# Fifth list tiles of two experts in one stage: 96 rows each, on four column groups of 32 and then on two halves

## The chip, the cores and the metric

The kernel runs on one core of one Trainium2 chip. A core has TensorE (matmuls, whose results go to PSUM banks), VectorE, ScalarE, GpSimd (POOL) and SyncE (SP), which work side by side and wait for each other by semaphores. Transfers are issued from SP's and POOL's queues. The metric is the device time of the whole kernel in microseconds (us); lower is better.

## The reference

The kernel computes two layers on 1024 tokens of 1024 channels. Layer 0 is a convolution-like attention with group norm, layer 1 is causal attention with 16 heads and then a mixture of 8 experts. The change is in the mixture alone:

```python
gate_logits = softmax(x @ gate_w + gate_b)
selected = (gate_logits >= THRESHOLD)            # 0.1
weights = gate_logits * selected
weights = weights / where(wsum == 0, 1, wsum)
for e in range(E):                               # 8 experts
    out = out + weights[:, e:e + 1] * (x @ expert_w[e] + expert_b[e])
```

`x` has 1024 rows, `expert_w[e]` is 1024 x 1024, all in f32. A token counts for an expert only where its gate is at least 0.1. With the reference's own inputs the experts get 560, 592, 542, 569, 578, 552, 545 and 538 of the 1024 tokens; of the first 896 tokens, experts 0 and 7 get 487 and 470.

## The kernel before

**Lists.** After the attention and the router, the kernel makes a list of token numbers for every expert (`gather`, `slot`, `add`, L693 to L695). It computes an expert only for the tokens on its list, in tiles of 128 entries. Five tiles are handled by the main path, `SLOTS = 5 * P` = 640 entries. Experts 0 and 7 (`SHORT`) have lists of the first 896 tokens, of which four tiles are handled; the last 128 tokens are computed for these two densely (`dense` L1135, `last_pe` L1207). If any list is longer (`most_i`, compared with `SLOTS` at L1219), a loop at the end computes what is left, all experts one after another. Unused entries at the end of a list point to tokens that aren't selected, with weight zero.

**One tile.** `get` / `fetch` (L712, L1060) issues four indirect gathers on POOL's queue, each bringing a quarter of a row into 128 partitions, into one of three `xg` buffers. `put` / `turn` (L724, L1063) transposes the tile on VectorE in blocks of 32. After the products, VectorE adds the bias, ScalarE multiplies by the gate weights, and `add_rows` (L743) issues an indirect transfer on POOL's queue that adds the rows to the output in DRAM.

**Pairs of tiles.** Tiles 0 and 1, and 2 and 3, are a pair of 256 rows. `products` (L1079) multiplies a pair by the expert's 1024 x 1024 weights with seven block products instead of eight (Strassen's scheme in Winograd's form). Each product is four matmuls of 128 x 128 by 128 x 512 (L1093). It needs sums of row blocks, `row_sums` (L1074, four VectorE operations, the last one in place: the block a21 becomes a11 - a21), and sums of weight blocks, which are made once per expert: `first_sum` and `second_sum` before its first pair, `third_sum` (in place in the weights: b12 becomes b22 - b12) and `fourth_sum` in it. The weights lie in two halves of 512 output columns, `w[e][0]` and `w[e][1]`; even and odd experts have buffers of their own (`w_even`, `w_odd`).

**The fifth tile.** For experts 1 to 6 the fifth tile has a stage of its own, `left_over` (L1117), between the products of the expert before and its own first pair. It multiplies the tile with the plain weights, in `weighted` (L731): for each half, eight matmuls of 128 x 128 by 128 x 512 (L737). It runs before `third_sum` changes the weights. While TensorE is in it, VectorE makes the fourth weight sum, the transpose of tile 1 and the row sums of the first pair.

**What sets the order.** This part is written out by hand (`manual_schedule`, L1126): the program order is each engine's order. `between` is a table of what is issued after the n-th product of a pair. So the stretch in which an expert's second pair is multiplied also transposes the next expert's first tiles and makes its first two weight sums. `load(e + 1)` is issued on SP's queue at the start of expert e, behind the stage `left_over(e)`, and waits there until the weights' buffers are free. A bias comes behind it, in the middle of the second pair, into one buffer. POOL's gathers and adds share one queue in program order.

Of the kernel before, what the change touches and what calls it, by code (L numbers as in the profile page):

```python
# [28 lines left out]
F32 = mybir.dt.float32  # L32
# [6 lines left out]
P = 128  # L39
# [18 lines left out]
NEG = -1e29  # L58
THRESHOLD = 0.1
Q = 4  # L60
SLOTS = 5 * P
SHORT = (0, E - 1)


# [1 line left out]
def kernel(  # L66
# [80 lines left out]
    def sums_of_A(a11, a12, a21, a22, s1, s2, s4):  # L147
        nc.vector.tensor_add(s1, a21, a22)
        nc.vector.tensor_sub(s2, s1, a11)
        nc.vector.tensor_sub(s4, a12, s2)  # L150
        nc.vector.tensor_sub(a21, a11, a21)

    def layer_norm(ln, t, dst):

# [300 lines left out]
    with ExitStack() as attention:  # L455
# [20 lines left out]
        def sums_of_B():  # L476
            nc.vector.tensor_sub(T[0], b12, b11)
            nc.vector.tensor_sub(T[1], b22, T[0])
            nc.vector.tensor_sub(b12, b22, b12)
            nc.vector.tensor_sub(T[2], b21, T[1])  # L480

        n_products = 0
# [221 lines left out]

        return w_tile(f"{name}{e}_{r}", expert_w[e][:, ts(r, HALF)], home=home)

    def expert_bias(e, home, name="w_e"):
        bias = home.tile([P, C], F32, tag="bias", name=f"{name}_bias{e}", bufs=1)
        nc.sync.dma_start(bias, expert_b[e].partition_broadcast(P))
        return bias  # L710

    def fetch(e, k, home, name="w_e", bufs=None):  # L712

        row = home.tile([P, Q, C // Q], F32, tag="xg", name=f"{name}_xg{e}_{k}", bufs=bufs)
        for g in range(Q):
            nc.gpsimd.indirect_dma_start(  # L716
                out=row[:, g, :],
                out_offset=None,
                in_=table[: (TOK - P) * Q, :] if e in SHORT else table,
                in_offset=bass.IndirectOffsetOnAxis(ap=gather[:, e, k * Q + g : k * Q + g + 1], axis=0),  # L720
            )
        return row

    def turn(row_T, row):  # L724

        nc.vector.transpose(  # L726
            row_T.rearrange("p c (g j) -> p g c j", g=Q),
            row.rearrange("p g (c i) -> p g c i", c=NC),
        )

    def weighted(gate, row_T, w, bias, home, name, between={}):  # L731
# [8 lines left out]
            nc.scalar.mul(y[:, ts(j, HALF)], y[:, ts(j, HALF)], gate)  # L740
        return y

    def add_rows(e, k, y):  # L743
        nc.gpsimd.indirect_dma_start(  # L744
            out=out[: TOK - P, :] if e in SHORT else out,
            out_offset=bass.IndirectOffsetOnAxis(ap=add[:, e, k : k + 1], axis=0),
            in_=y,
            in_offset=None,
            compute_op=ALU.add,
        )  # L750

    def by_rows(e, tiles, w, bias, home, name):

        tiles = list(tiles)

        def turned(k, row):
            row_T = home.tile([P, NC, P], F32, tag="row_T", name=f"{name}_xg_T{e}_{k}", bufs=3)
            turn(row_T, row)
            return row_T

        fetched = [fetch(e, k, home, name) for k in tiles[:2]]
        ready = [turned(tiles[0], fetched[0])]
        for n, k in enumerate(tiles):
            if n + 2 < len(tiles):
                fetched.append(fetch(e, tiles[n + 2], home, name))
            if n + 1 < len(tiles):
                ready.append(turned(tiles[n + 1], fetched[n + 1]))
            add_rows(e, k, weighted(slot[:, e, 1, k : k + 1], ready[n], w, bias, home, f"{name}{e}_{k}"))

    with ExitStack() as gating:  # L770
        l2, l2w = pool(gating, "l2"), pool(gating, "l2w", 2)
# [234 lines left out]
        def last_lists(entries):  # L1006
            read_lists(1, E, entries)


            pn = tr("pn")  # L1010
            nc.tensor.matmul(pn[:, :E], ones, kept, start=True, stop=True)
            need = l2.tile([P, E], F32, tag="need", name="need")
            nc.vector.tensor_copy(need, pn[:, :E])
            pn0 = tr("pn0")
            nc.tensor.matmul(pn0[:, :2], ones, kept_short, start=True, stop=True)
            nc.vector.tensor_scalar(need[:, :: E - 1], pn0[:, :2], float(P), None, ALU.add)
            most = l2.tile([P, 1], F32, tag="most", name="most")
            nc.vector.tensor_reduce(most, need, AX.X, ALU.max)
            nc.vector.tensor_copy(most_i, most)
# [11 lines left out]
        def half(e, j, l):  # L1031
            return w[e][l][:, 4 * j : 4 * j + 4, :]
# [15 lines left out]
        def third_sum(e):  # L1048

            T3[e] = half(e, 0, 1)  # L1050
            if e == E - 1:
                free = w_even.tile([P, NC, HALF], F32, tag="w", name="free")
                T3[e] = free[:, : NC // 2, :]
                last_rows.append(free[:, NC // 2 : NC // 2 + 2, :].rearrange("p a b -> p (a b)"))
            nc.vector.tensor_sub(T3[e], half(e, 1, 1), half(e, 0, 1))

        row = {}
        last = SLOTS // P - 1

        def get(e, k):  # L1060
            row[e, k] = fetch(e, k, two, bufs=3)

        def put(e, k):  # L1063

            if k == last:
                A[e, k] = l2w.tile([P, NC, P], F32, tag="row_T", name=f"one{e}", bufs=3)
                turn(A[e, k], row[e, k])
            else:
                pair, i = divmod(k, 2)
                if i == 0:  # L1070
                    A[e, pair] = two.tile([P, 2, NC, P], F32, tag="A", name=f"A{e}_{pair}")
                turn(A[e, pair][:, i, :, :], row[e, k])
# [6 lines left out]
        def products(e, pair, between):  # L1079
# [34 lines left out]
            rows_out(1, 0)  # L1114
            add_rows(e, 2 * pair + 1, y[1])

        def left_over(e):  # L1117

            between = {0: lambda: (fourth_sum(e), put(e, 1), get(e, 3)), 1: lambda: row_sums(e, 0)}
            get(e, 2)  # L1120
            y = weighted(slot[:, e, 1, last : last + 1], A[e, last], w[e], bias[e], l2w, f"one{e}", between)
            add_rows(e, last, y)

        with tc.manual_schedule():  # L1126
# [23 lines left out]
            )  # L1150
            get(0, 3)
            for e in range(E):
                if e not in SHORT:
                    left_over(e)
                if e + 1 < E:
                    load(e + 1)
# [6 lines left out]
                if e == 0:  # L1163
                    between[2] = lambda: (stage(3, NT - 1), fourth_sum(0), put(0, 2))
                    between[3] = lambda: (entries.append(copy_lists(1)), put(0, 3))
                    between[4] = lambda: (last_lists(entries[0]), row_sums(0, 1))
                    between.pop(1)
                elif e == E - 1:
                    between[0] = lambda: (third_sum(e), get(e, 3))
                    between[1] = lambda: (fourth_sum(e), put(e, 2))  # L1170
                if e + 1 < E - 1:
                    between[5] = lambda: get(e + 1, last)
                    between[6] = lambda: get(e + 1, 0)
                elif e + 1 == E - 1:
                    between[5] = lambda: get(e + 1, 0)
                    between[6] = lambda: get(e + 1, 1)
                products(e, 0, between)
                between = {}
                if e + 1 < E - 1:
                    between = {  # L1180
                        1: lambda: (bias.update({e + 1: expert_bias(e + 1, l2w)}), put(e + 1, last)),
                        2: lambda: (put(e + 1, 0), get(e + 1, 1)),
                        4: lambda: first_sum(e + 1),
                        5: lambda: second_sum(e + 1),
                        6: lambda: bias_step(e + 1),
                    }
                elif e + 1 == E - 1:
                    between = {
                        1: lambda: (bias.update({e + 1: expert_bias(e + 1, l2w)}), put(e + 1, 0), get(e + 1, 2)),
                        2: lambda: put(e + 1, 1),  # L1190
                        3: lambda: row_sums(e + 1, 0),
                        4: lambda: first_sum(e + 1),
                        5: lambda: second_sum(e + 1),
                        6: lambda: bias_step(e + 1),
                    }
                else:
                    between = {
                        1: lambda: nc.sync.dma_start(last_rows[0], out[ts(NT - 1, P), :]),
                        4: lambda: nc.vector.scalar_tensor_tensor(
                            last_rows[0], bias[e], gated[NT - 1][0][:, e, 1:2], last_rows[0], ALU.mult, ALU.add  # L1200
                        ),
                    }
# [16 lines left out]
    with tc.If(count > SLOTS), ExitStack() as rest:  # L1219
        w_rest, l3 = pool(rest, "w_rest", 4), pool(rest, "l3", 3)  # L1220
        for e in range(E):
            w_e = [half_weights(e, r, w_rest, "w_r") for r in range(2)]
            tiles = range(SLOTS // P - 1, NT - 1) if e in SHORT else range(SLOTS // P, NT)
            by_rows(e, tiles, w_e, expert_bias(e, l3, "w_r"), l3, "w_r")


# [57 lines left out]
```

## Time and profile before

| what | value |
| --- | --- |
| median of 3 runs | 1308.68 us (1306.49 to 1309.3) |
| the profiled execution, its own time | 1310.25 us |
| its span (first to last instruction) | 1308.4 us |
| TensorE busy | 1286.6 us, 98% |
| VectorE busy | 664.3 us, 51% |
| POOL busy | 344.3 us, 26% |
| ScalarE busy | 245.3 us, 19% |
| chain that ended last | TensorE 93%, VectorE 4%, rest 3% |
| the experts, first product to the end | from 821.8 us to the end of the span |
| fifth tiles on TensorE (L737, one_pe) | 83.4 us, 192 records |

A group's row gives line, engine, operation, result <- operands, shapes and count, then the time in which at least one of its instructions ran and the mean time of one, and then the idle time before them with what ended it. For a matmul, 128*32 is the stationary operand (128 partitions, 32 columns) and 128x512 what comes out of the moving columns. Times of one matmul contain its latency, and matmuls overlap: the busy time divided by the count is nearer to what one costs in a row of them. An f32 matmul leaves two records. In the timeline and the chain, the first column is the start in us from the start of the span and the second the length. The tiles `p` are the pairs' products, `one_pe` the fifth tile's, `w_e_xg` a gathered tile, `A` and `one` transposed ones, `S` and `T` the sums.

### The profile page before, as it was taken

To read this page: it belongs to the slowest core of one execution; us is meant where nothing else is said; L and a number is where in the kernel's file an instruction comes from. 1 tells how busy PE (TensorE), PEld (TensorE's weight loads), DVE (VectorE), ACT (ScalarE), POOL (GpSimd) and SP (SyncE) were. 2 spreads that over 40 slices of the span, in tenths; PEclk is the share of its full clock that TensorE was granted. 3 is DMA by queue.
4 is the path that set the end of the run, shared out by engine and by line. 5 is a ranking of instruction groups with operands and counts; after the bars stand their busy time and mean duration, and the time that the engine had idled before them with its cause. 6 is when DMAs were issued, how large, how long until landed. Compare 5 with 4: busy or idle time off the path is not lost.

```text
span 1308.4 us, 12324 instructions
## 1 busy us (share of the span) xinstructions
PE 1286.6 (98%) x4550; PEld 695.5 (53%) x4550; DVE 664.3 (51%) x1250; ACT 245.3 (19%) x572; POOL 344.3 (26%) x365
## 2 busy tenths in 40 slices
PE   9999999998999999999999998999999999999998
PEld 5445894777884555555554544444444444444443
DVE  5874220566323555554444755655646465555642
ACT  3200111330001333333323322111111111110110
POOL 0000060230000211111111113445454544453530
PEclk9999999998999999999999998999999999999999
DMA  9020023512201202010505215374757566555532
GB/s 350 2 65 17 1 76 92 203 65 81 65 18 46 65 1 65 1 65 1 193 17 196 96 65 201 73 220 115 214 124 190 147 164 174 145 165 140 111 75 58
DMA packets 61042, 136.12 MB, mean 104 GB/s; under 512 B 5905, under 2 KB 20257, under 8 KB 60977
## 3 DMA queue, kind: packets, MB, share of 16 engines
q1 hardware_dynamic: 47664, 94.32, 20.7%
q0 software_dynamic: 13312, 40.96, 14.4%
q8 instruction: 38, 0.62, 0.2%
q14 instruction: 28, 0.22, 0.1%
HBM read 97.51 MB, written 33.55 MB: 100 GB/s over the span
## 4 chain that ended last, share of the span: by engine, by line
PE 93%; DVE 4%; POOL 1%; DMA 1%; issue 1%; ACT 0%; DVEq 0%; ACTq 0%; POOLq 0%
PE p L1093 28%; PE pqk L489 15%; PE po L646 8%; PE pq L257 7%; PE pv L489 7%; PE one_pe L737 6%; PE pT L376 3%; PE py L441 2%; PE pk L319 2%; PE pc L340 2%; PE pv L401 2%; PE sc L573 2%; PE pst L617 2%; PE pa L627 2%; PE last_pe L1209 1%; POOL w_e_xg L716 1%
## 5 line engine op out<-in xcount | busy, mean ns | idle before, releaser
L716 POOL DMA_INDIRECT w_e_xg<-rows,gather x152 | 159.2, 1048 | 69.1 <-issue 42.0
L1093 PE MATMUL p<-w_e,A 128*128 128x512 f32 x368 | 164.6, 597 | 1.8 <-DVE slot L954 1.8
L605 POOL TENSOR_TENSOR s<-s,total 128x256 f32<-128x256 f32 x64 | 51.5, 826 | 346.4 <-DVE total L602 338.4
L1093 PEld LDWEIGHTS p<-w_e,A 128*128 128x128 f32 x368 | 70.4, 192 | 90.5 <-issue 88.6
L646 PE MATMUL po<-w_p,y_T 128*128 128x512 f32 x256 | 116.1, 598 | 0.0
L744 POOL DMA_INDIRECT out_dram<-y,add x32 | 60.8, 1899 | 205.7 <-ACT y L1099 133.1
L1093 PE MATMUL p<-T,S 128*128 128x512 f32 x256 | 112.7, 592 | 0.0
L1099 ACT ACTIVATE y<-y,slot 128x512 f32<-128x512 f32 x64 | 46.2, 722 | 341.3 <-DVE y L1107 172.5
L257 PE MATMUL pq<-w_q,xn 128*128 128x512 f32 x224 | 99.6, 596 | 1.4 <-DVE q_s L261 1.1
L489 PE MATMUL pqk<-ln,w_qk 128*128 128x512 f32 x192 | 85.0, 592 | 0.0
L737 PE MATMUL one_pe<-w_e,one 128*128 128x512 f32 x192 | 83.4, 592 | 0.0
L1093 PEld LDWEIGHTS p<-T,S 128*128 128x128 f32 x256 | 48.6, 190 | 60.8 <-issue 60.7
L646 PEld LDWEIGHTS po<-w_p,y_T 128*128 128x128 f32 x256 | 46.3, 190 | 49.1 <-issue 48.7
L257 PEld LDWEIGHTS pq<-w_q,xn 128*128 128x128 f32 x224 | 41.8, 190 | 51.8 <-issue 47.4
L726 DVE STREAM_TRANSPOSE A<-w_e_xg 128x1024 f32<-128x1024 f32 x32 | 39.7, 1241 | 51.4 <-DMA w_e_xg<-rows,gather 51.4
L737 PEld LDWEIGHTS one_pe<-w_e,one 128*128 128x128 f32 x192 | 36.5, 190 | 45.9 <-issue 45.7
L595 ACT ACTIVATE s<-s,top 128x256 f32<-128x256 f32 (+1 forms) x128 | 56.6, 443 | 18.1 <-DVE top L593 18.0
L489 PEld LDWEIGHTS pqk<-ln,w_qk 128*128 128x128 f32 x192 | 35.9, 190 | 42.1 <-issue 41.1
L489 PE MATMUL pqk<-T,S_qk 128*128 128x512 f32 x128 | 57.7, 593 | 0.0
L1093 PE MATMUL p<-w_e,S 128*128 128x512 f32 x128 | 57.5, 592 | 0.0
L1093 PE MATMUL p<-T,A 128*128 128x512 f32 x128 | 57.5, 592 | 0.0
L618 ACT COPY s_T<-pst 128x384 f32<-128x384 f32 x64 | 27.5, 481 | 157.6 <-PE pst L617 157.6
(256 smaller groups left out, 1801.0 us busy)
## 6 DMA issues: line engine op xcount, KB each, us to landing
w_e<-in_expert_w_dram SPq DMA_DIRECT2D x16, 2048.0 KB, 12.1
w_qk<-in_W_attnT_dram SPq DMA_DIRECT2D x8, 1024.0 KB, 6.4
xn<-in_xT_dram SPq DMA_DIRECT2D x8, 512.0 KB, 7.8
x_at<-in_x_dram SPq DMA_DIRECT2D x8, 512.0 KB, 7.1
w_v<-in_W_attnT_dram SPq DMA_DIRECT2D x2, 2048.0 KB, 11.8
x_rows<-x_at SPq DMA_DIRECT2D x8, 512.0 KB, 2.7
w_p<-in_W_projT_dram SPq DMA_DIRECT2D x2, 2048.0 KB, 8.4
xb<-x_rows SPq DMA_DIRECT2D x8, 512.0 KB, 6.8
```

The costliest lines, as they stand in the source:

```text
L257: nc.tensor.matmul(pq, xn[:, c, ts(t, P)], w_q[kc][:, c, :], start=(c == 0), stop=(c == NC - 1))
L376: nc.tensor.matmul(out_T[:, g, :, :], window[:, kc, :, :].rearrange("p i j -> p (i j)"), q0[:, kc, first : first + n_i, nj, :], start=(kc ...
L489: nc.tensor.matmul(bank, stationary(c), moving(c), start=(c == 0), stop=(c == NC // 2 - 1))
L595: nc.scalar.activation(s[:, h, cols], s[:, h, cols], AF.Exp, bias=top[:, qt, h : h + 1], accum_out=total[:, qt, h : h + 1],)
L605: nc.gpsimd.tensor_mul(s[:, :, cols], s[:, :, cols], total[:, qt, :].unsqueeze(2).to_broadcast([P, 2, (qt + 1) * P]),)
L646: nc.tensor.matmul(po, y_T[:, c, ts(t, P)], w_p[j][:, c, :], start=(c == 0), stop=(c == NC - 1))
L716: nc.gpsimd.indirect_dma_start(out=row[:, g, :], out_offset=None, in_=table[: (TOK - P) * Q, :] if e in SHORT else table, in_offset=bass.I ...
L726: nc.vector.transpose(row_T.rearrange("p c (g j) -> p g c j", g=Q), row.rearrange("p g (c i) -> p g c i", c=NC),)
L737: nc.tensor.matmul(pe, row_T[:, c, :], w[j][:, c, :], start=(c == 0), stop=(c == NC - 1))
L744: nc.gpsimd.indirect_dma_start(out=out[: TOK - P, :] if e in SHORT else out, out_offset=bass.IndirectOffsetOnAxis(ap=add[:, e, k : k + 1], ...
L1093: nc.tensor.matmul(bank, a[:, c, :], b[:, c, :], start=(c == 0), stop=(c == NC // 2 - 1))
L1099: nc.scalar.mul(y[i][:, ts(j, HALF)], y[i][:, ts(j, HALF)], slot[:, e, 1, 2 * pair + i : 2 * pair + i + 1])
```

## The change

The list part that the main path handles goes from 640 to 608 entries: the fifth tile has 96 rows instead of 128 (`LEFT`). Fifth tiles are no longer worked on by one expert each but by two, an odd one d and the even one e = d + 1 after it: experts 1 and 2, 3 and 4, 5 and 6. The stage stands between the products of d and those of e, so there are three stages instead of six, and odd experts go from the expert before straight to their first pair.

A stage has two parts. In the first, each chunk of 128 input channels gets four matmuls of 32 stationary columns, which write to four groups of 32 partitions of one bank: three have the 96 rows of d with d's weights, the fourth has the last 32 rows of e with e's weights. In the second, the other 64 rows of e are multiplied; the 1024 input channels are split into two halves that are written to the two halves of the partitions of a bank, and ScalarE and VectorE add them.

By then d's weights have been changed by `third_sum`. This is met by the algebra: the third sum is now b12 - b22, the in-place row sum a21 - a11 has its sign turned as well, so their product stays the same; and `sum_left` adds the two halves of d's fifth tile, so that a1 (b12 - b22) + (a1 + a2) b22 = a1 b12 + a2 b22.

What is issued when moves with it. Odd experts now get what experts without a fifth tile had: tiles 0 and 1 and the row sums are made in the second pair of the expert before, and the fourth weight sum, and the gather of tile 3, in their own first pair. Both fifth tiles are gathered in d's first pair and transposed in its second. Biases now have two buffers, and are issued ahead of the second pair. The loop for what is left over begins at the fifth tile and sets the weights of its first 96 entries to zero.

```diff
-SLOTS = 5 * P
+LEFT = 96
+SLOTS = 4 * P + LEFT
...
-        nc.vector.tensor_sub(a21, a11, a21)
+        nc.vector.tensor_sub(a21, a21, a11)
...
-            nc.vector.tensor_sub(T3[e], half(e, 1, 1), half(e, 0, 1))
+            nc.vector.tensor_sub(T3[e], half(e, 0, 1), half(e, 1, 1))
...
-            row[e, k] = fetch(e, k, two, bufs=3)
+            row[e, k] = fetch(e, k, two, bufs=3, slots=LEFT if k == last else P)
...
+        def sum_left(e):
+
+            A[e, "sum"] = l2w.tile([P, NC, P], F32, tag="row_T", name=f"sum{e}", bufs=3)[:, : NC // 2, :LEFT]
+            nc.vector.tensor_add(A[e, "sum"], A[e, last][:, : NC // 2, :LEFT], A[e, last][:, NC // 2 :, :LEFT])
+
         def left_over(e):
 
+            d = e - 1
             between = {0: lambda: (fourth_sum(e), put(e, 1), get(e, 3)), 1: lambda: row_sums(e, 0)}
             get(e, 2)
-            y = weighted(slot[:, e, 1, last : last + 1], A[e, last], w[e], bias[e], l2w, f"one{e}", between)
-            add_rows(e, last, y)
+            y_d, y_e = (l2w.tile([P, C], F32, tag="ye", name=f"left{e}_{i}", bufs=3) for i in range(2))
+
+            for j in range(2):
+                bank = (tr if j else mm)(f"left{e}_{j}")
+                for c in range(NC):
+                    a = A[d, last][:, c, :] if j == 0 or c < NC // 2 else A[d, "sum"][:, c - NC // 2, :]
+                    for i in range(Q):
+                        stationary, of = (a[:, ts(i, 32)], d) if i < Q - 1 else (A[e, last][:, c, 64:LEFT], e)
+                        nc.tensor.matmul(
+                            bank[ts(i, 32), :], stationary, w[of][j][:, c, :], start=(c == 0), stop=(c == NC - 1)
+                        )
+                between[j]()
+                y = y_d[:LEFT, ts(j, HALF)]
+                nc.vector.tensor_add(y, bank[:LEFT, :], bias[d][:LEFT, ts(j, HALF)])
+                nc.scalar.mul(y, y, slot[:LEFT, d, 1, last : last + 1])
+                nc.vector.tensor_add(y_e[64:LEFT, ts(j, HALF)], bank[LEFT:, :], bias[e][LEFT:, ts(j, HALF)])
+            add_rows(d, last, y_d, LEFT)
+
+            for j in range(2):
+                bank = (tr if j else mm)(f"rest{e}_{j}")
+                for c in range(NC // 2):
+                    for i in range(2):
+                        nc.tensor.matmul(
+                            bank[ts(i, 64), :],
+                            A[e, last][:, i * (NC // 2) + c, :64],
+                            w[e][j][:, i * (NC // 2) + c, :],
+                            start=(c == 0),
+                            stop=(c == NC // 2 - 1),
+                        )
+                other = two.tile([P, HALF], F32, tag="U", name=f"other{e}_{j}", bufs=5)
+                nc.scalar.copy(other[:64, :], bank[64:, :])
+                y = y_e[:64, ts(j, HALF)]
+                nc.vector.tensor_add(y, bank[:64, :], bias[e][:64, ts(j, HALF)])
+                nc.vector.tensor_add(y, y, other[:64, :])
+                y = y_e[:LEFT, ts(j, HALF)]
+                nc.scalar.mul(y, y, slot[:LEFT, e, 1, last : last + 1])
+            add_rows(e, last, y_e, LEFT)
...
-                if e not in SHORT:
+                if e % 2 == 0 and e:
                     left_over(e)
                 if e + 1 < E:
                     load(e + 1)
...
-                elif e == E - 1:
+                elif e % 2:
                     between[0] = lambda: (third_sum(e), get(e, 3))
                     between[1] = lambda: (fourth_sum(e), put(e, 2))
-                if e + 1 < E - 1:
-                    between[5] = lambda: get(e + 1, last)
-                    between[6] = lambda: get(e + 1, 0)
-                elif e + 1 == E - 1:
+                if e % 2 == 0:
                     between[5] = lambda: get(e + 1, 0)
                     between[6] = lambda: get(e + 1, 1)
+                elif e + 1 < E:
+                    between[5] = lambda: (get(e, last), get(e + 1, last))
+                    between[6] = lambda: get(e + 1, 0)
                 products(e, 0, between)
...
+                if e + 1 < E:
+                    bias[e + 1] = expert_bias(e + 1, l2w, tag="xg", bufs=2)
                     between = {
...
                         4: lambda: first_sum(e + 1),
                         5: lambda: second_sum(e + 1),
                         6: lambda: bias_step(e + 1),
                     }
...
+                if e % 2 == 0:
+                    between[1] = lambda: (put(e + 1, 0), get(e + 1, 2))
+                    between[2] = lambda: put(e + 1, 1)
+                    between[3] = lambda: row_sums(e + 1, 0)
+                elif e + 1 < E:
+                    between[1] = lambda: put(e, last)
+                    between[2] = lambda: (put(e + 1, last), sum_left(e))
+                    between[3] = lambda: (put(e + 1, 0), get(e + 1, 1))
```

More of the change, by code (lines that the diff above doesn't have):

```diff
@@ L478, in sums_of_B @@
             nc.vector.tensor_sub(T[1], b22, T[0])
-            nc.vector.tensor_sub(b12, b22, b12)
+            nc.vector.tensor_sub(b12, b12, b22)
             nc.vector.tensor_sub(T[2], b21, T[1])
@@ L705, in half_weights, with expert_bias, fetch @@
         return w_tile(f"{name}{e}_{r}", expert_w[e][:, ts(r, HALF)], home=home)
-    def expert_bias(e, home, name="w_e"):
-        bias = home.tile([P, C], F32, tag="bias", name=f"{name}_bias{e}", bufs=1)
+    def expert_bias(e, home, name="w_e", tag="bias", bufs=1):
+        bias = home.tile([P, Q, C // Q], F32, tag=tag, name=f"{name}_bias{e}", bufs=bufs).rearrange("p a b -> p (a b)")
         nc.sync.dma_start(bias, expert_b[e].partition_broadcast(P))
         return bias
-    def fetch(e, k, home, name="w_e", bufs=None):
+    def fetch(e, k, home, name="w_e", bufs=None, slots=P):
         row = home.tile([P, Q, C // Q], F32, tag="xg", name=f"{name}_xg{e}_{k}", bufs=bufs)
-        for g in range(Q):
+        for g in range(slots // 32):
             nc.gpsimd.indirect_dma_start(
@@ L722, in fetch, with turn @@
         return row
-    def turn(row_T, row):
+    def turn(row_T, row, slots=P):
         nc.vector.transpose(
-            row_T.rearrange("p c (g j) -> p g c j", g=Q),
-            row.rearrange("p g (c i) -> p g c i", c=NC),
+            row_T[:, :, :slots].rearrange("p c (g j) -> p g c j", j=32),
+            row[:, : slots // 32, :].rearrange("p g (c i) -> p g c i", c=NC),
         )
@@ L741, in weighted, with add_rows @@
         return y
-    def add_rows(e, k, y):
+    def add_rows(e, k, y, slots=P):
         nc.gpsimd.indirect_dma_start(
             out=out[: TOK - P, :] if e in SHORT else out,
-            out_offset=bass.IndirectOffsetOnAxis(ap=add[:, e, k : k + 1], axis=0),
-            in_=y,
+            out_offset=bass.IndirectOffsetOnAxis(ap=add[:slots, e, k : k + 1], axis=0),
+            in_=y[:slots, :],
             in_offset=None,
@@ L754, in by_rows, with gates @@
         tiles = list(tiles)
+        def gates(k):
+            if k > SLOTS // P or e in SHORT:
+                return slot[:, e, 1, k : k + 1]
+            late = home.tile([P, 1], F32, tag="late", name=f"{name}_late{e}")
+            nc.vector.memset(late, 0.0)
+            nc.vector.tensor_copy(late[LEFT:, :], slot[LEFT:, e, 1, k : k + 1])
+            return late
         def turned(k, row):
@@ L767, in by_rows @@
                 ready.append(turned(tiles[n + 1], fetched[n + 1]))
-            add_rows(e, k, weighted(slot[:, e, 1, k : k + 1], ready[n], w, bias, home, f"{name}{e}_{k}"))
+            add_rows(e, k, weighted(gates(k), ready[n], w, bias, home, f"{name}{e}_{k}"))
     with ExitStack() as gating:
@@ L1015, in last_lists @@
             nc.tensor.matmul(pn0[:, :2], ones, kept_short, start=True, stop=True)
-            nc.vector.tensor_scalar(need[:, :: E - 1], pn0[:, :2], float(P), None, ALU.add)
+            nc.vector.tensor_scalar(need[:, :: E - 1], pn0[:, :2], float(LEFT), None, ALU.add)
             most = l2.tile([P, 1], F32, tag="most", name="most")
@@ L1054, in third_sum @@
                 last_rows.append(free[:, NC // 2 : NC // 2 + 2, :].rearrange("p a b -> p (a b)"))
-            nc.vector.tensor_sub(T3[e], half(e, 1, 1), half(e, 0, 1))
+            nc.vector.tensor_sub(T3[e], half(e, 0, 1), half(e, 1, 1))
         row = {}
-        last = SLOTS // P - 1
+        last = SLOTS // P
         def get(e, k):
-            row[e, k] = fetch(e, k, two, bufs=3)
+            row[e, k] = fetch(e, k, two, bufs=3, slots=LEFT if k == last else P)
         def put(e, k):
@@ L1066, in put @@
                 A[e, k] = l2w.tile([P, NC, P], F32, tag="row_T", name=f"one{e}", bufs=3)
-                turn(A[e, k], row[e, k])
+                turn(A[e, k], row[e, k], LEFT)
             else:
@@ L1167 @@
                     between.pop(1)
-                elif e == E - 1:
+                elif e % 2:
                     between[0] = lambda: (third_sum(e), get(e, 3))
                     between[1] = lambda: (fourth_sum(e), put(e, 2))
-                if e + 1 < E - 1:
-                    between[5] = lambda: get(e + 1, last)
-                    between[6] = lambda: get(e + 1, 0)
-                elif e + 1 == E - 1:
+                if e % 2 == 0:
                     between[5] = lambda: get(e + 1, 0)
                     between[6] = lambda: get(e + 1, 1)
+                elif e + 1 < E:
+                    between[5] = lambda: (get(e, last), get(e + 1, last))
+                    between[6] = lambda: get(e + 1, 0)
                 products(e, 0, between)
-                between = {}
-                if e + 1 < E - 1:
+                if e + 1 < E:
+                    bias[e + 1] = expert_bias(e + 1, l2w, tag="xg", bufs=2)
                     between = {
-                        1: lambda: (bias.update({e + 1: expert_bias(e + 1, l2w)}), put(e + 1, last)),
-                        2: lambda: (put(e + 1, 0), get(e + 1, 1)),
                         4: lambda: first_sum(e + 1),
@@ L1186 @@
                     }
[L1187 to L1195, printed above, removed]
+                if e % 2 == 0:
[6 more added lines that the diff above has]
+                    between[3] = lambda: (put(e + 1, 0), get(e + 1, 1))
                 else:
@@ L1222 @@
             w_e = [half_weights(e, r, w_rest, "w_r") for r in range(2)]
-            tiles = range(SLOTS // P - 1, NT - 1) if e in SHORT else range(SLOTS // P, NT)
+            tiles = range(SLOTS // P, NT - 1 if e in SHORT else NT)
             by_rows(e, tiles, w_e, expert_bias(e, l3, "w_r"), l3, "w_r")
```

## Prediction

> **What bounds the kernel.** I read the page first for the bound, then the chain of waits in order of time for the place of the change, then the groups with shapes kept apart, the timeline and the windows for prices.
>
> ```profile
> PE 1286.6 (98%) x4550; PEld 695.5 (53%) x4550; DVE 664.3 (51%) x1250; ACT 245.3 (19%) x572; POOL 344.3 (26%) x365
> ```
>
> The chain that ended last, in order of time (start, length, engine, line, instructions), from expert 0's first pair on:
>
> ```profile
> 837.10 32.83 PE p L1093 x72
> 869.94 13.73 PE one_pe L737 x32
> 883.67 48.07 PE p L1093 x112
> 931.74 13.73 PE one_pe L737 x32
> ...
> 1178.94 13.73 PE one_pe L737 x32
> 1192.67 96.13 PE p L1093 x224
> 1288.80 13.75 PE last_pe L1209 x32
> ```
>
> From 837 us to the last matmul the chain is TensorE alone; only the last addition and its transfer follow. An expert is 48.07 us of products (2 calls x 7 products x 4 matmuls) and, for experts 1 to 6, 13.73 us of the fifth list tile (16 matmuls). Each f32 matmul leaves two records, so 13.73 / 32 = 0.429 us is one pass over 512 moving columns, and that is the unit below. TensorE sets the end of this stretch, so passes taken out of it come off the time unless another engine is late.
>
> **What the Trainium skill says.** "TensorE: Matmul & The Clock Gate", Part 3: Packing small matmuls, says that matmuls of 32 stationary columns in different column groups run at once, and gives 2.38x for three of them with 512 moving columns, less than the ideal 3. "TensorEngine Tiling (Array Packing)", Key Properties: "Changing tiling mode (not just tile) drains the TensorE". The trace of before has both. The groups view and the timeline around one gate of the router:
>
> ```profile
> L319 PE MATMUL pk<-w_kv,xn 128*64 128x256 f32 x256 | 27.9, 380 | 0.0
> L852 PE MATMUL parts<-row_T,gw 128*32 128x128 f32 x128 | 5.8, 296 | 0.0
> ```
>
> ```profile
> 713.74 1.02 PE L646 MATMUL po<-w_p,y_T 128*128 128x512 f32 x2
> 714.69 0.65 PE L852 MATMUL parts<-row_T,gw 128*32 128x128 f32 x16
> 715.27 1.13 PE L646 MATMUL po<-w_p,y_T 128*128 128x512 f32 x2
> ```
>
> L319 works on two halves of 64: 27.9 / 256 = 0.109 us a record at 256 columns, where half a unit would be 0.215 us: two truly run at once. L852 works on four groups of 32 with four different moving operands: 16 records in 0.65 us, of which the last one's own latency is 0.27 us. The single start times in the trace are fours about 7 ns apart, a four every 0.109 us after a first step of 0.134 us. 128 columns cost a quarter of a unit, 0.107 us, for one matmul alone; here they cost that for four. So the trace is better than the page's 2.38 of 3, and I take four at once, one unit a round. What it does not show is four groups with 512 columns.
>
> The drain shows too: the first L852 record starts 0.522 us after the L646 record before it instead of 0.429 (+0.093); the way back costs 0.202 instead of 0.109 (+0.093), and the next start comes after 0.534 instead of 0.429 (+0.105).
>
> **The change, part by part.**
>
> *Removed.* Six one_pe stages of 32 units: 6 x 13.73 = 82.4 us of TensorE, all on the path. Also 6 gathers of 1.05 us on POOL (19 instead of 20 for each of experts 1 to 6) and 12 additions and 12 scalings, which were hidden.
>
> *Added on TensorE, three times.* Four groups: 2 halves x 8 chunks x 4 matmuls, in rounds of four with two passes each: 32 rounds = 13.73 us. Two halves: 2 x 4 x 2 matmuls, rounds of two: 16 rounds = 6.87 us. Together 20.60 us where two experts took 27.46: 6.86 us saved, three times 20.6 us. Against it three mode switches a stage: 0.093 + 0.025 into four groups, 0.093 + about 0.08 into two halves (L319's first step is 0.327 instead of 0.216 us, the attention's L627 0.267 instead of 0.216; I take the middle), 0.093 + 0.105 back: 0.49 us, three times 1.5 us. Bounds of the switches: 0.3 us if the two column modes change over free, 1 us if each costs twice what it does here.
>
> *Bounds of the round with 512 columns.* Below: 0.429 us, the array's rate; a gain beyond is excluded. Above: two at a time, 0.858 us. By the page's 2.38 of 3 it would be 1.26 units, 0.54 us (an estimate). I take 0.429 us, since L852 kept its rate over four rounds running, which are together as long as one round of 512.
>
> *ScalarE* gets two copies of 64 rows a stage beside its four scalings of 0.72 us: under 5 us in 20.6, hidden.
>
> *VectorE.* Odd experts lose the 13.73 us in which transposes, the fourth weight sum and the row sums used to run, and keep the work. For an odd expert from single durations in the timeline: four weight sums 4 x 2.28, transposes of its tiles 2 and 3 and of the next expert's tile 0 3 x 1.24, two of 96 rows about 0.93 each (three quarters of 1.24), one set of row sums 2.75, the new sum of halves about 0.52, the bias step 0.68, 18 additions x 0.69: 31 us in 48.07. An even one has 30 us in 48.07, and its stage 12 us in 20.6. Before:
>
> ```profile
> core 0: us, PE busy (x) PEld busy (x) DVE busy (x) ACT busy (x) POOL busy (x), PEclk, DMA share, GB/s
> 883.60:931.70 48.10, 48.10 (x114) 21.31 (x113) 26.71 (x30) 5.78 (x8) 26.33 (x22) 1.00 0.57 156
> 1116.90:1130.70 13.80, 13.80 (x33) 6.08 (x32) 7.35 (x8) 1.44 (x2) 4.84 (x5) 1.00 0.81 208
> 1192.60:1240.70 48.10, 48.10 (x114) 21.31 (x113) 29.17 (x34) 5.77 (x8) 24.65 (x20) 1.00 0.41 92
> ```
>
> The last row is expert 6 preparing expert 7, which has no fifth tile: the order that experts 1, 3 and 5 now get. TensorE is busy all of it. So it costs nothing there. The narrowest place is expert 0 to 1, where lists come late:
>
> ```profile
> 860.68 1.25 DVE L726 STREAM_TRANSPOSE A<-w_e_xg 128x1024 f32<-128x1024 f32 x1 [7.12 <-DMA w_e_xg<-rows,gather]
> ...
> 866.54 2.28 DVE L1039 TENSOR_TENSOR T<-w_e,T 128x2048 f32<-128x2048 f32 x1
> ```
>
> The transpose at 860.68 had waited for the second set of four gathers after the lists. Now that POOL place holds tile 1 of expert 1, at the same time, and the row sums (2.75 us) come between. The second weight sum then ends at 868.8 + 2.75 = 871.6 us. Expert 1's third product, the first to need it, starts at 869.9 + 2 x 3.43 = 876.8 us. So 5 us are left. If they are gone, each us later is a us on the end.
>
> *POOL.* An odd expert issues 18 gathers at 1.05 + 0.30 us less some (1.26 us apart in the timeline) and 4 adds at 1.9 + 0.3: 31.5 us in 48. The six gathers of two fifth tiles stand ahead of the next expert's tile 0, 7.6 us. They start some 21 us into the expert, after the add of the first rows, so tile 0 has landed by about 21 + 12.6 + 6.6 (from the last issue to landing at 860.7) = 40 us, and its transpose is placed at 24 + 4 x 3.43 = 38 us: VectorE waits some 2 us. What is queued behind are additions that empty banks TensorE needs only 7 us later.
>
> *SP and DMA.* Weights of an odd expert now wait for the four-group stage, which still reads the previous odd one: half 0 is free 6.9 us into the stage, half 1 after 13.7. They are needed by the first weight sum, 20.6 + 24.0 + 17.2 = 62 us into it. A half takes 12.1 us to land: over 30 us of slack. The bias queued behind them is needed after that sum. Even experts' weights keep their time.
>
> *The rest loop* is taken over 608 list entries instead of 640. By the reference's own inputs the longest list has 592 (experts 0 and 7: 487 and 470 of the first 896 tokens, plus 96, which is 583 and 566), so it stays out.
>
> *Sum against the profiled execution:* span 1308.4 - 20.6 + 1.5 = 1289.3 us. The median of the runs shown, 1308.68, is 0.3 us above the span (the profiled execution's own time, 1310.25, is 1.8 above): 1289.5 us. Runs of before scatter from 1306.49 to 1309.3, so 0.2%, 2.6 us, is about what can be told from no change.
>
> **Rivals.**
> 1. *Clean gain*, 1288 to 1291 us: above. Chance 0.74.
> 2. *Late rows or sums.* An odd expert runs out of cover at a junction (the 5 us at expert 0 to 1, or late gathers), and TensorE waits 1 to 7 us in all: 1291 to 1297 us. For: VectorE waited for gathers 51 us in all, and now 13.73 us of TensorE cover are gone before each odd expert. Against: expert 6 to 7 above. Chance 0.14.
> 3. *Four groups run below rate* with 512 columns, near the page's 1.26 units: 96 rounds x 0.11 us = 10.7 us of the gain gone: 1300 us. For: page only. Against: L852. Chance 0.06.
> 4. *Slower: only two groups at once.* In the four-group stage a round then takes 0.858 us, the stage 27.46 instead of 13.73: three times 13.73 = 41.2 us lost against a gain of 19.1: 1330.7 us. It decides from 0.63 us a round on (0.429 + 19.1 / 96). For: in an f32 matmul two passes follow each other, and if the second held the queue up only neighbours would overlap; L319 looks the same either way. Against: the fours of L852, also f32. Chance 0.05.
> 5. *No change to be told*, a mixture of 2 and 3 that eats 17 us or more: 0.01.
>
> **How the numbers follow.** Predicted is rival 1. The range 1287 to 1297 us holds cases 1 and 2, 0.88, less some edges; the lower end is switches at nothing and a run-to-run 0.1%. Faster: 0.74 + 0.14 + 0.06 = 0.94; same 0.01; slower 0.05.
>
> **What would show it.** In the profile after: L1145 with 192 matmuls (384 records) in three stretches of 13.7 to 14 us, fours starting together every 0.429 us; L1159 with 48 matmuls (96 records) in stretches of 6.9 us; the expert products still 0.429 us a record with no wait; VectorE's and POOL's waits longer for odd experts and not in the chain. Wrong if the rounds of L1145 are longer than 0.45 us, if TensorE waits for row sums, weight sums or transposes ahead of experts 1, 3 or 5, or if the change made anything else longer, since all instructions up to expert 0's second pair keep their order.

## The result

The changed kernel takes 1291.55 us (median of 4 runs, 1290.33 to 1293.02) where the kernel before took 1308.99 (4 runs, 1306.49 to 1311.0): a ratio of 0.9868, 95% interval 0.9848 to 0.9888. Predicted were 1289.5 us, a ratio of 0.985, within 1287 to 1297. It is faster by clearly more than 0.2%. A later set of runs (the first experiment) gives 0.9854, 0.9836 to 0.9873.

The profiled execution of the changed kernel has a span of 1288.5 us, 19.9 less than before. From its page:

```profile
PE 1266.1 (98%) x4838; PEld 676.3 (52%) x4838; DVE 670.3 (52%) x1265; ACT 248.7 (19%) x578; POOL 336.7 (26%) x359
```

TensorE's busy time fell by 20.5 us, and TensorE is still 98% busy: what was taken out of it is gone from the end. The chain of waits in order of time (start, length, engine, line, instructions):

```profile
836.19 80.90 PE p L1103 x184
917.09 13.87 PE left L1145 x128
930.96 7.02 PE rest L1159 x32
937.98 96.33 PE p L1103 x224
1034.31 13.87 PE left L1145 x128
...
1172.42 96.33 PE p L1103 x224
1268.75 13.75 PE last_pe L1257 x32
```

As before it is TensorE alone from 836 us to the last matmul. A stage is 13.87 + 7.02 us. Two experts' products behind it are 96.33 us where 2 x 48.07 = 96.13 stood before: the way back from the halves costs 0.20. So a stage is 21.09 us against 2 x 13.73 = 27.46, 6.37 us less, three times 19.1 us. From the start of the first product (815.0 us before, not the 821.8 of the table ahead, and 814.1 after) to that of the last one the traces show the same 19.1 us: 473.2 against 454.1. The other 0.8 us between the two spans lie outside this stretch, nearly all ahead of it. The two programs do the same work there, but for the signs of some subtractions and a constant, so I take them as scatter: the kernel before alone ranges over 6 us (1306.66 to 1312.6 in the first experiment).

The groups with shapes kept apart show the two column modes, with the same length of a record:

```profile
L1145 PE MATMUL left<-w_e,one 128*32 128x512 f32 x312 | 41.8, 593 | 0.0
L1145 PE MATMUL left<-w_e,sum 128*32 128x512 f32 x72 | 10.8, 592 | 0.0
L1159 PE MATMUL rest<-w_e,one 128*64 128x512 f32 x96 | 21.3, 595 | 0.0
L728 DVE STREAM_TRANSPOSE A<-w_e_xg 128x1024 f32<-128x1024 f32 x32 | 39.6, 1239 | 58.4 <-DMA w_e_xg<-rows,gather 58.4
L728 DVE STREAM_TRANSPOSE one<-w_e_xg 128x768 f32<-128x768 f32 x6 | 5.9, 978 | 17.0 <-DMA w_e_xg<-rows,gather 17.0
```

384 records of L1145 in 41.8 us (the `sum` ones share it in time) would be 0.109 us each; four at once make a round of 0.429 us, the length of one full-width pass. The single starts in the trace are fours, 6 to 7 ns apart, every 0.429 us from the second round to the last (the first step is 0.453). Those of L1159 are twos, as close together, every 0.429 us after a first step of 0.48. The transposes now wait for gathers 75.4 us in all, against 52.9 before (51.4 and 1.5 for the fifth tiles). TensorE doesn't: its one wait in the products is the 1.8 us at the lists (L964), as before.

### The profile page after: what moved, and what is told of

The parts are those of the page before. It is cut to its first block, busy times and chain, and to the rows that moved or that the text cites. A ratio compares the mean times of both kernels' runs of the same rounds, so it can differ in the third digit from the quotient of the medians.

```text
span 1288.5 us, 12902 instructions
## 1 busy us (share of the span) xinstructions
PE 1266.1 (98%) x4838; PEld 676.3 (52%) x4838; DVE 670.3 (52%) x1265; ACT 248.7 (19%) x578; POOL 336.7 (26%) x359
## 4 chain that ended last, share of the span: by engine, by line
PE 93%; DVE 4%; DMA 1%; POOL 1%; issue 1%; ACT 0%; DVEq 0%; POOLq 0%; ACTq 0%
PE p L1103 29%; PE pqk L491 15%; PE po L648 8%; PE pq L259 7%; PE pv L491 7%; PE left L1145 3%; PE pT L378 3%; PE py L443 2%; PE pk L321 2%; PE pc L342 2%; PE pv L403 2%; PE sc L575 2%; PE pst L619 2%; PE pa L629 2%; PE rest L1159 2%; PE last_pe L1257 1%
## 5 line engine op out<-in xcount | busy, mean ns | idle before, releaser
L718 POOL DMA_INDIRECT w_e_xg<-rows,gather x146 | 156.1, 1069 | 67.4 <-issue 40.5
L746 POOL DMA_INDIRECT out_dram<-y,add x32 | 57.0, 1782 | 175.5 <-ACT y L1109 114.2
L259 PEld LDWEIGHTS pq<-w_q,xn 128*128 128x128 f32 x224 | 41.8, 190 | 51.8 <-issue 47.4
L620 ACT COPY s_T<-pst 128x384 f32<-128x384 f32 x64 | 27.5, 481 | 157.6 <-PE pst L619 157.6
L491 PE MATMUL pv<-w_v,ln 128*128 128x256 f32 x192 | 43.8, 381 | 0.0
L1145 PE MATMUL left<-w_e,one 128*32 128x512 f32 x312 | 41.8, 593 | 0.0
```

The costliest lines, as they stand in the source:

```text
L259: nc.tensor.matmul(pq, xn[:, c, ts(t, P)], w_q[kc][:, c, :], start=(c == 0), stop=(c == NC - 1))
L491: nc.tensor.matmul(bank, stationary(c), moving(c), start=(c == 0), stop=(c == NC // 2 - 1))
L718: nc.gpsimd.indirect_dma_start(out=row[:, g, :], out_offset=None, in_=table[: (TOK - P) * Q, :] if e in SHORT else table, in_offset=bass.I ...
L746: nc.gpsimd.indirect_dma_start(out=out[: TOK - P, :] if e in SHORT else out, out_offset=bass.IndirectOffsetOnAxis(ap=add[:slots, e, k : k ...
L1145: nc.tensor.matmul(bank[ts(i, 32), :], stationary, w[of][j][:, c, :], start=(c == 0), stop=(c == NC - 1))
```

## Experiments

The theory: TensorE alone sets the end of this stretch, four column groups run at once at the full rate, and all that was moved is hidden. Rivals: the saving comes from the fewer rows or the new order; the groups don't run at once beyond two; another engine takes part of the gain. The first two kernels below were run several times, the others once each; of these, lengths are read from the traces.

### The gain once more

No edit; run again beside the kernel before.

> The changed kernel once more, unaltered, for the size of the gain. Theory (TensorE alone pays, 6.57 us saved in each of three stages by the trace, 19.7 us): 0.985 of the time before, some 1289.5 us where before is 1309. Rival (the medians shown so far, 1291.55 against 1308.99, 17.4 us: some 2 us of the gain are given back outside the profiled execution): 0.987.

Measured: 1291.1 us (median of 4, 1289.2 to 1291.87) against 1309.71 (23 runs): 0.9854, interval 0.9836 to 0.9873. The theory's ratio. Its 19.7 us left out the 0.20 us on the way back of each stage; it is 19.1 us, 0.9854 of 1308.7. The 2 us that the first runs seemed to give back are inside their interval.

### All of the change but the packing

```diff
-            for j in range(2):
-                bank = (tr if j else mm)(f"left{e}_{j}")
-                for c in range(NC):
...
-                    for i in range(Q):
-                        stationary, of = (a[:, ts(i, 32)], d) if i < Q - 1 else (A[e, last][:, c, 64:LEFT], e)
...
-                bank = (tr if j else mm)(f"rest{e}_{j}")
...
+            for of, y_of in ((d, y_d), (e, y_e)):
+                for j in range(2):
+                    bank = (tr if j else mm)(f"left{e}_{of}_{j}")
+                    for c in range(NC):
+                        a = A[of, last][:, c, :LEFT]
+                        if of == d and j == 1 and c >= NC // 2:
+                            a = A[d, "sum"][:, c - NC // 2, :]
+                        nc.tensor.matmul(bank[:LEFT, :], a, w[of][j][:, c, :], start=(c == 0), stop=(c == NC - 1))
...
```

> The new order of gathers, transposes and sums and the 96-row tiles are kept, but a stage multiplies d's and e's 96 rows one after the other with stationary operands of 96 columns, no groups. Theory (only the packing saves time; the smaller tile and the moved work are worth nothing): 64 passes of 0.429 us a stage, 27.5 us instead of 20.9, and the three switches gone: 1288.5 + 19.7 = 1308 us, no different from before. Rival (a part of the gain comes from fewer gathers and rows or the new order): 1290 to 1304 us. Rival (96 columns cost three quarters of 128): 1288 us.

Measured: 1309.26 us against 1309.71, ratio 0.9997, interval 0.9989 to 1.0005. Its chain, and the group:

```profile
915.84 27.47 PE left L1146 x64
943.31 96.13 PE p L1103 x224
1039.44 27.47 PE left L1146 x64
```

```profile
L1146 PE MATMUL left<-w_e,one 128*96 128x512 f32 x168 | 73.1, 592 | 0.0
```

64 records of 0.429 us, as with 128 columns: a stationary operand of 96 columns costs what one of 128 does. Six gathers less, the smaller transposes, the new order of everything on VectorE, POOL and SP, two biases: together nothing that can be measured, by the interval at most some 0.1%. The gain is the packing's.

### What makes groups run at once

Four kernels change only the order of the same 64 matmuls of the four-group stage.

```diff
-                for c in range(NC):
+                for i2, c, i1 in ((i2, c, i1) for i2 in range(2) for c in range(NC) for i1 in range(2)):
...
-                    for i in range(Q):
+                    for i in (2 * i2 + i1,):
```

> The four-group stage in another order: groups 0 and 1 for all eight chunks, then groups 2 and 3. Same matmuls. Theory (a group runs beside its neighbours in program order only, so now two at once): the stage takes 64 rounds of 0.429 us, 27.5 us instead of 13.9, and the span grows by 3 x 13.7 = 41 us to 1330. Rival (TensorE takes matmuls ahead in its queue, or the gain isn't from groups running at once): 1288 to 1291 us.

```diff
-                for c in range(NC):
+                for i, c in ((i, c) for i in range(Q) for c in range(NC)):
...
-                    for i in range(Q):
+                    for i in (i,):
```

> The four-group stage group by group: all eight chunks of group 0, then of group 1, and so on. Same matmuls. Theory: one at a time, 128 rounds of 0.429 us a stage, 54.9 us instead of 13.9, and the span grows by 3 x 41.2 = 123 us to about 1412. Rival (matmuls of another group are taken ahead): less than that, down to 1289.

Measured: spans of 1311.7 and 1375.8 us, from the chains of the two kernels:

```profile
914.38 22.55 PE left L1145 x128
936.93 7.02 PE rest L1159 x32
```

```profile
916.41 43.24 PE left L1145 x128
959.65 7.02 PE rest L1159 x32
```

The pairs lie between theory and rival; the groups one by one miss the theory too and fall into the wide range of its rival. The order does decide, so the gain is from groups running at once. But the pairs take 22.55 us instead of 27.5 and the groups one by one 43.24 instead of 54.9. Counted by single starts, they have 52 rounds instead of 64 and 100 instead of 128: each border between blocks saves exactly 4 rounds (3 borders in the first, 7 in the second). TensorE's weight loads of the one-by-one kernel, in the timeline, show what happens at a border; a line merges loads that touch:

```profile
921.08 0.11 PEld L1145 LDWEIGHTS left<-w_e,one 128*32 128x32 f32 x1 [0.32 <-issue]
921.51 0.14 PEld L1145 LDWEIGHTS left<-w_e,one 128*32 128x32 f32 x3 [0.32 <-issue]
921.94 0.14 PEld L1145 LDWEIGHTS left<-w_e,one 128*32 128x32 f32 x2 [0.29 <-issue]
922.37 0.14 PEld L1145 LDWEIGHTS left<-w_e,one 128*32 128x32 f32 x2 [0.29 <-issue]
922.83 0.11 PEld L1145 LDWEIGHTS left<-w_e,one 128*32 128x32 f32 x1 [0.32 <-issue]
```

At 921.51 the second group starts, and for three more rounds two run side by side: group 0 still has three of its 16 records to start when the first record of group 1, later in the program, starts. (The expectations below say four; that is with the one that starts together with it.) The trace doesn't name the group of a record, so this is counted from the starts. In the second half of a stage it can be seen by name: a group's last eight records read `sum`, and the first ones of the next group read `one`. One of `one` starts at 942.24 us, ahead of three of `sum` at 942.66, 943.09 and 943.52. With pairs it is the same for each group of a pair, six records in all, so it isn't one store of a fixed length for all. The new theory: records go out in program order, but each column group holds some of its own. Two more orders test it:

```diff
-                for c in range(NC):
+                for c, i in ((c, i) for c0 in range(0, NC, 2) for i in range(Q) for c in range(c0, c0 + 2)):
...
-                    for i in range(Q):
+                    for i in (i,):
```

> The four-group stage in blocks: two chunks (four records) of group 0, two of group 1, of 2, of 3, then the next two chunks. New theory, from the two orders before (a later group's first record started when four records of each group ahead of it were still waiting): each column group holds some four records waiting of its own, so program order matters only beyond that. Then blocks of four records cost nothing: a stage of 13.9 us, span 1288 to 1291. Rival (only neighbours in program order run together): two at a time at the borders of blocks at best, 41 us or more a stage, some 1370 us.

The next is the same with 4 in place of 2.

> Blocks of four chunks (eight records). With four records waiting per group, a block begins four records after the one before it, so two groups run at once on average: 16 blocks of 4 records' distance, the last one 8 long, 68 x 0.429 = 29.2 us a stage, and a span of 1288.5 + 3 x 15.3 = 1334 us. Rival (a larger store shared by the groups): less than 25 us a stage. Rival (only neighbours in program order): over 40 us.

Measured: spans of 1289.9 and 1336.9 us, from the chains:

```profile
918.44 13.94 PE left L1145 x128
932.38 7.02 PE rest L1159 x32
```

```profile
917.52 29.75 PE left L1145 x128
947.28 7.02 PE rest L1159 x32
```

Both as expected: blocks of four records cost 0.07 us a stage, blocks of eight 15.9. The starts of a new block are 1.747 us apart in the trace of the second, 4.07 rounds; 15 of them and 8 rounds are 29.6 us. All four orders fit a group that takes one record at work and three waiting, where a fifth one for the same group holds up all that comes after it in the program; what holds them is not shown. It would also explain why the two passes of an f32 matmul, which follow each other in the same group, don't keep the next group from starting.

### How much cover is left

The narrowest place was predicted at expert 0 to 1. In the changed kernel the second weight sum ends there at 869.3 us:

```profile
867.03 2.28 DVE L1049 TENSOR_TENSOR T<-w_e,T 128x2048 f32<-128x2048 f32 x1
```

Two kernels make the second weight sum of expert 1 two or four times more, which only costs VectorE time:

```diff
-                        4: lambda: first_sum(e + 1),
+                        4: lambda: (first_sum(e + 1), [second_sum(e + 1) for _ in range(4 if e == 0 else 0)]),
```

> VectorE makes the second weight sum of expert 1 twice more ahead of the real one's place, 2 x 2.20 = 4.4 us of work at the narrowest junction, expert 0 to 1. Theory (6.6 us of slack there by the trace of the changed kernel: the sum ends at 869.3 us, the product that needs it starts at 875.9): no wait of TensorE, span as without, 1288 to 1291. Rival (VectorE already sets the end there): 4.4 us more.

> The same sum four times more, 8.8 us. Theory: 6.6 us are hidden, TensorE waits 2.2 us ahead of expert 1's third product, and the rest of the trace shifts by that. Rival (the slack is larger since other engines give way): no wait. Rival (no slack): 8.8 us.

Measured: 1290.0 and 1292.2 us. With two sums, the chain from expert 0 on has the same lengths as without. With four, TensorE waits at the third product of expert 1. The sum that it waits for, and the windows around it:

```profile
875.68 2.28 DVE L1049 TENSOR_TENSOR T<-w_e,T 128x2048 f32<-128x2048 f32 x1
```

```profile
core 0: us, PE busy (x) PEld busy (x) DVE busy (x) ACT busy (x) POOL busy (x), PEclk, DMA share, GB/s
869.00:876.00 7.00, 6.43 (x15) 2.49 (x14) 6.93 (x5) 0.20 (x1) 0.00 (x0) 1.00 0.66 252
876.00:879.00 3.00, 0.98 (x1) 0.50 (x2) 2.91 (x3) 0.52 (x1) 2.20 (x1) 0.78 0.00 0
879.00:882.50 3.50, 3.50 (x7) 1.58 (x6) 3.50 (x4) 1.44 (x2) 0.46 (x1) 0.70 0.78 119
882.50:890.00 7.50, 7.50 (x19) 3.30 (x18) 4.79 (x5) 0.72 (x1) 4.54 (x4) 1.00 0.42 66
```

The next record starts 3.18 us after the one before it instead of 0.43, so TensorE lost 2.75 us, 0.55 more than the theory's 2.2. The price of the extra sums was too low, not the slack: they follow each other every 2.33 us, not 2.20, and put the real sum off by 9.3 us. It ended at 877.97 us. Without them it would have ended at 868.7 (an estimate: in the changed kernel it ends 5.1 us after the first sum starts, which is at 863.58 here), and the product was due at 875.3, 6.6 us after that. With two sums 2.0 us were left of it.

The granted clock (PEclk) is at 0.70 over the 3.5 us from 879.0. In windows of 1 us it is 0.83 from 877, still in the wait, 0.50 from 878 to 881 and 0.96 after that. Four records stand 0.60 to 1.01 us apart, 1.6 us more than four times 0.429. A wait of 2.75 us cost 4.4 here. The slack is there, of the size read from the trace, and beyond it a wait can cost more than its length. It needn't: the three kernels with short stages below have six waits of 3.0 us between them, ahead of the first product behind the second and the third stage. After three of them the granted clock is 0.63 to 0.72 over the next 3 us, after the other three it is 1.00.

A third kernel makes the stage itself short and leaves the rest as it is:

```diff
-                for c in range(NC):
+                for c in (NC - 1,):
...
-                for c in range(NC // 2):
+                for c in (NC // 2 - 1,):
...
```

> The stages are cut to one chunk of the channels: a stage has 4 rounds on four groups and 4 on two halves instead of 32 and 16. The rest of the sum over channels is left out for the fifth tiles; everything else stays. Theory (TensorE alone sets the end, VectorE and POOL have cover to spare): 40 rounds less in each of three stages, 3 x 17.2 = 51.5 us off, 1237 us. Rival (VectorE's 13.5 us of a stage, or the gathers queued behind, become the bound once the stage is only 3.7 us long): TensorE waits in the next expert's first pair, up to 10 us a stage, 1240 to 1267 us.

Measured: 1269.0 us, 19.5 off instead of 51.5. It is a little beyond the rival's range, on the side of more waiting: 17.2 us less of matmuls in a stage bring 6.5. TensorE's starts later than 0.56 us after the one before sum up to 29 us of waits from expert 1 on, all of them ahead of first products, of products that need the second weight sum, and of the second half-stage. POOL's timeline behind one such stage shows what may be one reason:

```profile
947.53 1.51 POOL L746 DMA_INDIRECT out_dram<-left,add  x1 [0.30 <-issue]
953.61 1.44 POOL L746 DMA_INDIRECT out_dram<-left,add  x1 [4.56 <-issue]
959.64 1.57 POOL L746 DMA_INDIRECT out_dram<-y,add  x1 [4.59 <-issue]
961.51 1.01 POOL L718 DMA_INDIRECT w_e_xg<-rows,gather  x1 [0.30 <-issue]
```

Three adds in a row stand 6 us apart, about the time an add takes to land (6.4 us in the profile of before), and the gathers of the next expert's tiles queue behind them. The transposes' wait for gathers rose from 75.4 to 140.8 us. Two last runs test that reason: the short stage without the fifth tiles' adds, and the short stage again beside it. Beside the short stage's own edit, the first of them leaves out two lines:

```diff
-            add_rows(d, last, y_d, LEFT)
...
-            add_rows(e, last, y_e, LEFT)
```

> The cut stages of the run before that (one chunk of the channels), and the fifth tiles' rows are not added to the output either: six fewer adds on POOL's queue. It tells why 17.2 us less matmuls in a stage gave only 6.5. Theory (POOL's program order: an add waits for the add before it to land, three stand in a row around a short stage, and the gathers of the next expert's tiles queue behind them): with two of the three gone, TensorE's waits for transposed tiles shrink and the span falls from 1269.0 by 10 us or more, towards 1237. Rival (VectorE's own work, or the landing of gathers beside the weights' transfers, is what is late): 1265 to 1269 us.

> The cut stages once more, beside the run without the adds on the same chip: 1269 us as before, within 2 us.

Measured: 1259.4 us without the adds, 1271.6 beside it with them: 12.2 us less, or 9.6 against the first run of the short stage, which is at the edge of what the theory asked for. The repeat is 2.6 us above the first, not within 2; it has one wait of 6.0 us ahead of a first product that the other run doesn't have.

Part of these differences lies ahead of the experts and is scatter. From the first product to the last, where the changed kernel takes 454.1 us, the short stage takes 432.8 and 435.0 us, and 425.7 without the adds: 7 to 9 us less, from one run against two that differ by 2.2. So the adds are part of it, about a quarter of the 30 us that are missing. In the repeat's trace, the adds behind the stage start 0.8 us after the landing of the one before (951.72 and 952.52, 957.71 and 958.46), so adds do go one at a time. The run doesn't tell this from the rest that goes with the adds, their traffic and the buffers that they hold.

The other 20 us or more stay open between POOL's gathers, their landing beside the weights' transfers and VectorE's own work; without the adds the transposes still wait 132 us for gathers. None of this stands in the changed kernel's way, but it shows what comes next: of a stage 17.2 us shorter only 6.5 us are gained. From which length on TensorE starts to wait was not measured.

## Why the prediction was right

- *Round of four groups with 512 columns, 0.429 us*: right. It came from the 128-column groups of the router, not from the 2.38 of 3 in the Trainium skill ("TensorE: Matmul & The Clock Gate", Part 3: Packing small matmuls). The page has three groups, this kernel four in a long row, and here the measurement decides: 64 matmuls in four groups took 13.87 us where one group after another, with no overlap, would take 54.9, which is 3.96 of 4.
- *Switches, 0.49 us a stage*: the sum is right to the hundredth: 13.87 - 13.73, 7.02 - 6.87 and 96.33 - 96.13 are 0.14, 0.15 and 0.20. That is in part luck: the first two were put at 0.12 and 0.17, and the errors cancel. The drain on a change of mode ("TensorEngine Tiling (Array Packing)", Key Properties) shows at all three borders: 0.52 us from one start to the next instead of 0.43.
- *Net 19.1 us*: 19.1 us in the chain, and 0.9854 in the second set of runs. The first set gave 0.9868, 2 us less, inside its interval.
- *VectorE hidden*: right. Estimated were 31 us for an odd expert, 30 for an even one and 12 for a stage; expert 1's stretch had 28.1 busy in 48.07, expert 2's products 29.8, and the stage between them 14.1 in 20.9. The junction from 0 to 1 had 6.6 us left, not 5: counted from the start of expert 0's stretch at 836 or 837 us, the transpose of tile 1 began 1.3 us earlier than the one at its place before (858.51 and 860.68).
- *POOL*: the size was off. Gathers of the two fifth tiles and of tile 0 were put some 21 us into an odd expert; in expert 1 they began 28 us in. The transposes of the three tiles waited 5.6, 1.8 and 2.8 us, where I had named some 2 us for tile 0 alone. The term that was missed: the transpose of tile 3 holds VectorE, at 887.4 after a wait of 8.7 us, and with it the additions of the third to fifth products, so the first add of rows, and all gathers behind it on POOL, came 7 us later. It was covered: the fifth tiles were ready 9 us ahead of their stage.
- *SP, DMA, rest loop*: no wait of TensorE for them shows, and the loop didn't run.
- *Rival of two groups at once*: excluded by the result. Its price, 0.858 us a round and 27.46 us a stage, holds where the order leaves two at once: with blocks of eight records the stage took 29.75 us, with one group alone in the first and last four of 68 rounds. What decides is the order of the matmuls, which the prediction took as given: in the order of pairs, 1311.7 us, the whole gain is gone.

## What to carry to other kernels

When two remainders each fill a part of the array, count 32-column groups over both and put them side by side, even with different weights: in this kernel time follows full-width rounds, and a smaller tile alone saves nothing. Alternate the groups in program order: up to four records of one group in a row cost nothing here, eight halved the rate. Take the rate from what the trace already shows for the same kind of packing; here it was nearer than a general figure. Before removing cover from another engine, find the one junction where its work is late and compare the end of the sum with the start of the product that needs it: that number, 6.6 us here, held when it was tested. Price the added work as it runs in a row; that was the term that was off in the test.

## What was not expected of the hardware

A column group took records ahead on its own: a later group's record started while three records of an earlier group, ahead of it in the program, were still waiting. Blocks of four records per group ran at the full rate (13.94 us a stage), blocks of eight at about half of it (29.75), blocks of sixteen at a third (43.24). The limit is per group, since with pairs six records waited and in blocks of four as many as nine. And with a wait of 2.75 us the granted clock fell to 0.50 for some 3 us, which added 1.6 us to it, while after three of six waits of 3.0 us it stayed at 1.00.
